# Row sums of attention brought to queries on partitions by 32-column products with four columns of the identity, in a step of their own

## The chip, the cores and the metric

The kernel runs on one core of one Trainium2 chip. The metric is the device time of one execution in microseconds (us): the median over the runs shown. A page of one profiled execution and its trace stand beside it.

## The reference, cut to what matters

Sixteen graphs (B = 16), each with 1024 nodes of 256 features and an integer adjacency matrix, pass through two layers. The first is a graph transformer with masked self-attention of 8 heads of 32 features, in which queries, keys and values are the same normalized rows; the second is a graph attention layer with one score per pair of nodes. Cut to the part around the change:

```
h = relu(layernorm(x))
n = layer_norm(h, gamma1, beta1)              # queries = keys = values, 8 heads of 32
scores = einsum("bhqd,bhkd->bhqk", n, n) / sqrt(32)
attn = softmax(where(adj > 0, scores, -inf))  # over k
h = h + einsum("bhqk,bhkd->bhqd", attn, n)    # heads side by side again
x = x + h + gelu(layer_norm(h, gamma2, beta2) @ W1 + b1) @ W2 + b2
...                                           # then the second layer
```

The softmax's division is what the change touches: for every query and head, the weighted sum of values is divided by the row sum of the exponentials.

## The kernel before, in words

The path that runs here is `fast_path`. It is one long program without loops on the chip: Python generators emit the instructions of all sixteen graphs, and the order in which they are emitted is the order on each engine. `streams` holds six generators (attention, the MLP and second layer, preparation, loading of the next graph, masks, set-up), and the one with the least place goes next. While the attention of graph `b` runs, the MLP and the second layer of graph `b - 1` are emitted in between, a piece of some 1.75 us of TensorE's work at a time. `defer` sets a step aside until a clock of emitted work (`clock`) has passed a due time; `run_deferred` emits what is due.

Attention is done in units `(qh, g, kt)`: `qh` is a half of the queries (512), `g` a group of four heads, `kt` a block of 128 keys. A unit's scores stand transposed, keys on partitions and queries along the row: `scores` (L952) makes four heads' scores in PSUM, VectorE adds the mask (L973), ScalarE takes the exponential (L976). In the next unit `weigh` (L989) multiplies the exponentials with the values into `o`, where the four heads' 32 features lie on 128 partitions and the queries along the row. A DMA that adds (L1013) sums the exponentials over the key blocks.

After the eight key blocks of one `(g, qh)`, three steps follow, each in a later call of `go_on`, so that each has some microseconds to spare:

- `weigh` ends with a copy of `o` to `os` on VectorE (L1004);
- `total` multiplies the summed exponentials with ones (L901), which puts each head's row sums on 32 equal partitions of `den`, and ScalarE copies it to `ds` (L909);
- `finish` brings both to queries on partitions: four transposes of 128x128 of `ds` and four of `os` (L922), into two PSUM tiles `ptds` and `ptos`; a reciprocal of one column per head (L925), a product of outputs and reciprocals (L927) and an addition to `h` on GpSimd (L929).

`finish` is not called by `go_on` itself: it is put on the list `turns`, together with other transposes (of keys, `ptk`; of MLP inputs, `pty`; of second-layer inputs, `ptf`), with the number of PSUM tiles that it takes. `make_turns`, at the start of each unit, runs what there is room for:

```
was_totalled -> turns.append((2, lambda args=args: finish(*args)))
room = 3 - open_sums[0] - bool(summed) if open_sums[0] else 100
```

All these tiles, and those of the MLP and the second layer (`ph`, `po`, `pf`, `pa`, `pg`, `puT`, `lg`), come from one PSUM pool, `psm`, with three buffers; `open_sums` is 1 while a product that is only half summed holds one of them over a unit. A tile that is asked for takes the buffer that came free first, and its first instruction waits for the engine that read that buffer last.

Most products are made in quarters: `matmul` (L570) splits the 128 columns of the stationary operand into four of 32, each with its own 32 partitions of the output, and the four run side by side. Scores, `o` and `den` are split by hand into 64 and 32 columns. Only the transposes take the array whole, 128 by 128. The set-up makes two products of one moving column each, `p_w_a`, in the same quarters.

There are 16 x 2 x 2 = 64 calls of `finish`.

Of the kernel before, what the change touches and what calls it, by code (L numbers as in the profile page):

```python
# [9 lines left out]
F32 = mybir.dt.float32  # L10
# [6 lines left out]
P = 128  # L17
# [476 lines left out]
def fast_path(  # L494
# [28 lines left out]
    nc = tc.nc  # L523
    B, N, D = x.shape
    DFF = W1.shape[1]
    H, HD = 8, D // 8
    GH = 4
# [6 lines left out]
    TPH = QW // P  # L534
# [6 lines left out]
    const = pool("const", 1)  # L541
# [11 lines left out]
    smallp = pool("smallp", 3)  # L553
# [4 lines left out]
    def ps_tile(shape, name, dtype=F32):  # L558
        return psm.tile(shape, dtype, tag="ps", name=name)
# [36 lines left out]

    ident = const.tile([P, P], F32, name="ident")
    make_identity(nc, ident)
    ident8 = const.tile([P, P], FP8, name="ident8")
    nc.vector.tensor_copy(ident8, ident, saturate=False)  # L600
    ones = const.tile([P, HD], F32, name="ones")
# [131 lines left out]
    clock = [0.0]  # L733
    deferred = []

    def defer(us, f):
        deferred.append((clock[0] + us, len(deferred), f))

        return clock[0] + us

    def run_deferred(until=0.0):
        while True:
            due = [d for d in deferred if d[0] <= max(until, clock[0])]
            if not due:
                return
            d = min(due, key=lambda d: d[:2])
            deferred.remove(d)
            d[2]()
# [132 lines left out]
    turns = []  # L881

    open_sums = [0]

    def make_turns():
        room = 3 - open_sums[0] - bool(summed) if open_sums[0] else 100
        while turns and turns[0][0] <= room:
            n, f = turns.pop(0)
            room -= n
            f()  # L890
# [3 lines left out]
    scored, weighed, summed, totalled = [], [], [], []  # L894

    def total(b, qh, g, os, accs):

        den = ps_tile([P, QW], f"den_{b}_{g}_{qh}")
        for j in range(GH):
            for acc in accs:  # L900
                nc.tensor.matmul(  # L901
                    den[j * HD : (j + 1) * HD, :],
                    ones,
                    acc[j // 2][:, j % 2, :],
                    start=acc is accs[0],
                    stop=acc is accs[-1],
                )
        ds = tmpp.tile([P, QW], F32, tag="w2", bufs=3, name=f"ds_{b}_{g}_{qh}")
        nc.scalar.copy(ds, den)  # L909
        totalled.append((b, qh, g, ds, os))  # L910

    finished = {}

    def finish(b, qh, g, ds, os):
        h = hs[b]
        finished[b, qh] = finished.get((b, qh), 0) + 1
        clock[0] += 1.0
        pts = []
        for n, c in (("ds", ds), ("os", os)):
            pt = ps_tile([P, TPH, P], f"pt{n}_{b}_{g}_{qh}")  # L920
            for t in range(TPH):
                nc.tensor.transpose(pt[:, t, :], c[:, t * P : (t + 1) * P], ident)  # L922
            pts.append(pt.rearrange("p t (j d) -> p t j d", d=HD))
        rl = smallp.tile([P, TPH, GH], F32, tag="rl", name=f"rl_{b}_{g}_{qh}")
        nc.vector.reciprocal(rl, pts[0][:, :, :, 0])  # L925
        ot = tmpp.tile([P, TPH, GH, HD], F32, tag="w2", bufs=3, name=f"ot_{b}_{g}_{qh}")
        nc.vector.tensor_mul(ot, pts[1], rl.unsqueeze(3).to_broadcast([P, TPH, GH, HD]))  # L927
        ho = h[qh][:, :, g * P : (g + 1) * P]
        nc.gpsimd.tensor_add(ho, ho, ot.rearrange("p t j d -> p t (j d)"))  # L929

    def attention(b, st):
# [84 lines left out]
        for u in units:  # L1016
            make_turns()
            es, rest_of_weights = scores(*u)
            go_on()
            rest_of_weights()  # L1020
            qh, g, kt = u
            if kt == 0:
                sums[g, qh] = es
            else:
                for i in range(2):
                    defer(2.0 + 1.5 * i, lambda u=u, e=es[i], i=i: add_up(*u, e, i))
            scored.append((weigh, (*u, es)))
            yield

    def go_on():  # L1030
        was_weighed, was_summed, was_totalled = weighed[:], summed[:], totalled[:]
        for l in (weighed, summed, totalled):
            l.clear()
        if scored:
            f, args = scored.pop()
            f(*args)
        summed.extend(was_weighed)
        for args in was_summed:
            total(*args)
        for args in was_totalled:  # L1040
            turns.append((2, lambda args=args: finish(*args)))
        clock[0] += 2.0

    def close_attention():
        for _ in range(4):
            make_turns()
            go_on()
            yield
        make_turns()
        quarters[0] = False  # L1050
# [436 lines left out]
def kernel(tc, x, adj, gamma1, beta1, *rest):  # L1487
    nc = tc.nc
    D = x.shape[2]
    with tc.tile_pool(name="flags", bufs=1) as flags:  # L1490
        flag = flags.tile([1, 1], I32, name="bounded")
        redo = flags.tile([1, 1], I32, name="redo")
        with tc.tile_pool(name="bound", bufs=1) as pool:
            r = pool.tile([1, 2, D], F32, name="bound_rows")
            for i, src in enumerate((gamma1, beta1)):
                nc.sync.dma_start(
                    r[:, i, :], bass.AP(tensor=src.tensor, offset=src.offset, ap=[[0, 1], [1, D]])
                )
            m = pool.tile([1, 2], F32, name="bound_max")
            nc.vector.tensor_reduce(  # L1500
                m, r, axis=mybir.AxisListType.X, op=ALU.max, apply_absolute_value=True
            )
            s = pool.tile([1, 1], F32, name="bound_sum")
            nc.vector.tensor_scalar_mul(s, m[:, 1:2], math.sqrt(32.0))
            nc.vector.scalar_tensor_tensor(s, m[:, 0:1], 16.0, s, op0=ALU.mult, op1=ALU.add)
            nc.vector.tensor_scalar(
                flag, s, math.sqrt(BOUND * math.sqrt(32.0)), None, op0=ALU.is_le
            )
        nc.vector.tensor_scalar(redo, flag, -1.0, 1.0, op0=ALU.mult, op1=ALU.add)
        bounded = nc.values_load(flag[0:1, 0:1], min_val=0, max_val=1)  # L1510
        with tc.If(bounded > 0):
            fast_path(tc, x, adj, gamma1, beta1, *rest, redo)
        again = nc.values_load(redo[0:1, 0:1], min_val=0, max_val=1)
        with tc.If(again > 0):
            general_path(tc, x, adj, gamma1, beta1, *rest)
# [28 lines left out]
```

## Time and profile before

| What | us |
|---|---|
| median of three runs | 3492.38 (3491.94 to 3497.32) |
| the profiled execution | 3488.4 |
| its span, first to last instruction | 3486.6 |
| TensorE (PE) busy | 3432.9 |
| VectorE (DVE) busy | 2759.6 |
| ScalarE (ACT) busy | 1858.0 |
| GpSimd (POOL) busy | 1415.0 |
| `ptds` transposes, 256 instructions, busy | 42.0 |
| `ptos` transposes, 256 instructions, busy | 38.8 |
| reciprocals L925, 64 | 15.9 |
| products L927, 64 | 44.3 |

PE is TensorE's matrix products and PEld its loads of stationary operands, which run under the products. An fp32 product leaves two records of each kind, a transpose one. "128*32" in a row is the part of the array that is used, rows by columns. The busy time of a group counts overlapped instructions once; the mean of one is its own duration. Idle time has the name of the instruction whose end released it, or "issue" where the profile shows no wait. All durations are of the one profiled execution.

### The profile page before, as it was taken

The numbers are of one execution on the slowest core, as the hardware profiler recorded it, in microseconds if no ns is written. First come the engines' busy times: TensorE is split into PE (matmuls) and PEld (weight loads), VectorE is DVE, ScalarE is ACT, GpSimd is POOL, SyncE is SP. The second block draws the span as 40 slices with busy tenths as digits, with TensorE's granted clock in tenths as the row PEclk, the third lists the DMA queues.
The fourth block names the chain that finished last, engine by engine and source line by source line (L and its number), as shares of the span: only waits on it lengthen the run. The fifth ranks groups of instructions, "written<-read, shape, count | busy, mean of one in ns | idle before, by whom it ended". The sixth has DMA issues, their size and how long they took to land.

```text
span 3486.6 us, 115512 instructions
## 1 busy us (share of the span) xinstructions
PE 3432.9 (98%) x50686; PEld 1634.1 (47%) x50686; DVE 2759.6 (79%) x5193; ACT 1858.0 (53%) x2184; POOL 1415.0 (41%) x1708
## 2 busy tenths in 40 slices
PE   6999999999999999999999999999999999999998
PEld 2244444444444444444444444444444444444477
DVE  6888788787877877888887887878878788887754
ACT  4555555555555555555555555555555555555522
POOL 3443443434434344443444534344344443534220
PEclk9999999999999999999999999999999999999999
DMA  7699989999899998989989899998999989899720
GB/s 186 148 184 165 189 165 186 181 191 187 163 186 175 191 181 169 182 171 189 196 170 182 168 185 186 184 188 160 190 177 192 185 165 182 169 190 184 148 62 14
DMA packets 281892, 598.33 MB, mean 172 GB/s; under 512 B 94882, under 2 KB 130084, under 8 KB 281380
## 3 DMA queue, kind: packets, MB, share of 16 engines
q0 software_dynamic: 124416, 453.04, 71.0%
q1 hardware_dynamic: 154276, 134.41, 15.1%
q8 instruction: 400, 6.55, 0.8%
q10 hardware_dynamic: 2688, 3.41, 0.3%
q14 instruction: 112, 0.92, 0.1%
HBM read 104.21 MB, written 16.78 MB: 35 GB/s over the span
## 4 chain that ended last, share of the span: by engine, by line
PE 91%; DMA 3%; DVE 3%; issue 1%; ACT 0%; POOL 0%; SPq 0%; ACTq 0%; POOLq 0%; DVEq 0%
PE s L952 15%; PE o L989 13%; PE pa L570 12%; PE ph L570 11%; PE po L570 11%; PE lg L570 10%; PE pg L570 3%; PE puT L570 3%; PE pf L570 3%; DMA acc<-e 2%; PE den L901 2%; PE pty L1119 1%; PE ptf L1195 1%; PE ptk L801 1%; PE pa L567 1%
## 5 line engine op out<-in xcount | busy, mean ns | idle before, releaser
L976 ACT ACTIVATE e<-e 128x1024 f32<-128x1024 f32 x852 | 896.1, 1057 | 958.7 <-DVE e L973 722.2
L1013 POOL DMA_DIRECT2D acc<-e x864 | 756.1, 892 | 1433.8 <-DMA acc<-e 635.4
L973 DVE TENSOR_TENSOR e<-s,mk 128x1024 f32<-128x1024 f32 x852 | 1002.4, 1217 | 181.0 <-PE s L952 153.2
L952 PE MATMUL s<-kT 32*64 32x512 f32 x8192 | 579.9, 616 | 4.0 <-DVE odd L973 3.2
L989 PE MATMUL o<-e,va 128*32 128x512 f32 x3456 | 461.8, 605 | 2.1 <-ACT e L976 2.1
L570 PE MATMUL pa<-gw,e 128*32 128x258 f32 x7648 | 453.4, 380 | 0.0
L570 PE MATMUL lg<-fT,uT 128*32 128x256 f32 x7680 | 447.4, 379 | 0.0
L570 PE MATMUL ph<-yT,w 128*32 128x256 f32 x7808 | 446.4, 379 | 0.0
L570 PE MATMUL po<-w,hid 128*32 128x256 f32 x7680 | 439.0, 379 | 0.0
L570 PEld LDWEIGHTS ph<-yT,w 128*32 128x32 f32 x7808 | 255.3, 110 | 211.7 <-issue 50.7
L570 PEld LDWEIGHTS pa<-gw,e 128*32 128x32 f32 x7648 | 249.7, 110 | 210.9 <-issue 56.7
L570 PEld LDWEIGHTS po<-w,hid 128*32 128x32 f32 x7680 | 250.1, 110 | 209.1 <-issue 58.5
L570 PEld LDWEIGHTS lg<-fT,uT 128*32 128x32 f32 x7680 | 250.0, 110 | 208.6 <-issue 43.4
L1243 DVE SCALAR_TENSOR_TENSOR e<-lg,gw,mk 128x256 f32<-128x256 f32 x512 | 223.0, 477 | 71.6 <-PE lg L570 61.1
L1249 ACT ACTIVATE e<-e,shift 128x512 f32<-128x512 f32 x256 | 182.9, 717 | 179.9 <-DVE e L1248 124.4
L1146 DVE TENSOR_TENSOR hid<-ph,b1c 128x512 f32<-128x512 f32 x256 | 175.9, 687 | 89.0 <-PE ph L570 77.4
L989 PEld LDWEIGHTS o<-e,va 128*32 128x32 f32 x3456 | 68.6, 108 | 353.6 <-issue 201.7
L976 ACT ACTIVATE acc<-acc 128x1024 f32<-128x1024 f32 x124 | 131.0, 1057 | 130.0 <-DVE acc L973 125.6
L1248 DVE SCALAR_TENSOR_TENSOR e<-e 128x512 f32<-128x512 f32 x256 | 191.9, 750 | 8.8
L952 PEld LDWEIGHTS s<-kT 32*64 32x64 f32 x8192 | 120.9, 130 | 164.8 <-issue 118.3
L973 DVE TENSOR_TENSOR acc<-s,mk 128x1024 f32<-128x1024 f32 x124 | 146.0, 1218 | 16.8 <-PE s L952 16.7
L793 POOL TENSOR_TENSOR nrm<-nrm,g 128x256 f32<-128x256 f32 x128 | 112.6, 880 | 62.8 <-DVE nrm L727 62.8
(145 smaller groups left out, 3825.5 us busy)
## 6 DMA issues: line engine op xcount, KB each, us to landing
acc<-e POOLq DMA_DIRECT2D x864, 512.0 KB, 6.1
adj<-in_adj_dram SPq DMA_DIRECT2D x248, 256.0 KB, 5.4
h<-in_x_dram SPq DMA_DIRECT2D x64, 256.0 KB, 5.8
xb<-in_x_dram SPq DMA_DIRECT2D x128, 128.0 KB, 4.9
out_dram<-z SPq DMA_DIRECT2D x128, 128.0 KB, 3.8
adj<-in_adj_dram SPq DMA_DIRECT2D x4, 512.0 KB, 7.0
mk<-mq SPq DMA_TRANSPOSE x128, 6.2
w<-in_L_gnn_W_dram ACTq DMA_DIRECT2D x2, 1024.0 KB
```

What stands on the lines that cost most here:

```text
L570: nc.tensor.matmul(out[c : c + HD], lhsT[:, c : c + HD], rhs, start=start, stop=stop)
L793: nc.gpsimd.tensor_mul(nrm, nrm, g1)
L901: nc.tensor.matmul(den[j * HD : (j + 1) * HD, :], ones, acc[j // 2][:, j % 2, :], start=acc is accs[0], stop=acc is accs[-1],)
L952: nc.tensor.matmul(sc[j // 2][c : c + P // 2, j % 2, :], kT[r, g, kt * P + c : kt * P + c + P // 2], kT[r, g, qs], start=j >= by_pe, stop= ...
L973: nc.vector.tensor_tensor(e, masked, mb, op=ALU.add)
L976: weights = lambda e=e, masked=masked: nc.scalar.activation(e, masked, AF.Exp, scale=SCALE)
L989: nc.tensor.matmul(o[j * HD : (j + 1) * HD, :], va[:, kt, (g * GH + j) * HD : (g * GH + j + 1) * HD], es[j // 2][:, j % 2, :], start=(kt = ...
L1013: nc.gpsimd.dma_start(sums[g, qh][i], e, accum_op=ALU.add)
L1146: nc.vector.tensor_tensor(hid[:, f0 : f0 + 2, :], ph, b1c[:, f0 : f0 + 2].unsqueeze(2).to_broadcast([P, 2, CW]), op=ALU.add,)
L1243: nc.vector.scalar_tensor_tensor(e[:, j, :], lg[:, j, :], gw[:, kt, D : D + 1], st[c // 2][:, kt // 2, qs, kt % 2], op0=ALU.add, op1=ALU.add,)
L1248: nc.vector.scalar_tensor_tensor(e, e, ALPHA, e, op0=ALU.mult, op1=ALU.max)
L1249: ready = defer(2.5, lambda: nc.scalar.activation(e, e, AF.Exp, bias=shift))
```

## The change

A constant `each_head` is added: columns 0, 32, 64 and 96 of the identity. `finish` is parted in two. `invert`, called straight from `go_on`, multiplies `ds` with `each_head` in 16 products, four per block of 128 queries: the stationary operand is 32 columns of `ds`, the moving one has four columns. The result holds, for 128 queries on partitions, the row sums of four heads side by side (the 32 equal partitions of each head are not summed: a column of `each_head` picks one). Its PSUM tile has 4 x 4 columns where there were 4 x 128. The reciprocal is set aside for 1.0 us of the clock. What is left of `finish`, the transposes of `os` and what follows, goes to `turns` and takes one PSUM tile.

```
+    each_head = const.tile([P, GH], F32, name="each_head")
+    nc.vector.tensor_copy(each_head, ident[:, ::HD])
...
-        room = 3 - open_sums[0] - bool(summed) if open_sums[0] else 100
+        room = 3 - open_sums[0] - bool(summed or totalled) if open_sums[0] else 100
...
-    def finish(b, qh, g, ds, os):
+    def invert(b, qh, g, ds, os):
+
+        pt = ps_tile([P, TPH, GH], f"ptds_{b}_{g}_{qh}")
+        for t in range(TPH):
+            for c in range(0, P, HD):
+                nc.tensor.matmul(
+                    pt[c : c + HD, t, :], ds[:, t * P + c : t * P + c + HD], each_head, start=True, stop=True
+                )
+        rl = smallp.tile([P, TPH, GH], F32, tag="rl", name=f"rl_{b}_{g}_{qh}")
+        ready = defer(1.0, lambda: nc.vector.reciprocal(rl, pt))
+        turns.append((1, lambda: finish(b, qh, g, rl, ready, os)))
+
+    def finish(b, qh, g, rl, ready, os):
         h = hs[b]
+        run_deferred(ready)
         finished[b, qh] = finished.get((b, qh), 0) + 1
-        clock[0] += 1.0
-        pts = []
-        for n, c in (("ds", ds), ("os", os)):
-            pt = ps_tile([P, TPH, P], f"pt{n}_{b}_{g}_{qh}")
-            for t in range(TPH):
-                nc.tensor.transpose(pt[:, t, :], c[:, t * P : (t + 1) * P], ident)
-            pts.append(pt.rearrange("p t (j d) -> p t j d", d=HD))
-        rl = smallp.tile([P, TPH, GH], F32, tag="rl", name=f"rl_{b}_{g}_{qh}")
-        nc.vector.reciprocal(rl, pts[0][:, :, :, 0])
+        clock[0] += 0.5
+        pt = ps_tile([P, TPH, P], f"ptos_{b}_{g}_{qh}")
+        for t in range(TPH):
+            nc.tensor.transpose(pt[:, t, :], os[:, t * P : (t + 1) * P], ident)
         ot = tmpp.tile([P, TPH, GH, HD], F32, tag="w2", bufs=3, name=f"ot_{b}_{g}_{qh}")
-        nc.vector.tensor_mul(ot, pts[1], rl.unsqueeze(3).to_broadcast([P, TPH, GH, HD]))
+        nc.vector.tensor_mul(
+            ot, pt.rearrange("p t (j d) -> p t j d", d=HD), rl.unsqueeze(3).to_broadcast([P, TPH, GH, HD])
+        )
...
         for args in was_totalled:
-            turns.append((2, lambda args=args: finish(*args)))
+            invert(*args)
```

In the order of instructions, the 64 groups of 16 products stand one piece of work (some 3.5 us of TensorE's) earlier than the transposes that they replace, right behind the unit's `o` products; the `os` transposes stay where they were. On VectorE the 64 reciprocals stand some instructions earlier. The other engines' instructions and their order are the same.

## The prediction

> **What bounds the kernel now.** I read the page's busy table first, then the chain that ended last, then the busy times by stretch.
>
> ```profile
> PE 3432.9 (98%) x50686; PEld 1634.1 (47%) x50686; DVE 2759.6 (79%) x5193; ACT 1858.0 (53%) x2184; POOL 1415.0 (41%) x1708
> ...
> PE 91%; DMA 3%; DVE 3%; issue 1%; ACT 0%; POOL 0%; SPq 0%; ACTq 0%; POOLq 0%; DVEq 0%
> ```
>
> TensorE is busy for 98% of the span and carries 91% of the chain. By stretches it is clearer still (columns: window, its length, busy time of PE, weight loads, DVE, ACT, POOL, granted clock, DMA share, GB/s):
>
> ```profile
> 215.00:3270.00 3055.00, 3050.64 (x46768) 1425.32 (x46768) 2474.66 (x4630) 1669.24 (x1956) 1288.67 (x1544) 1.00 0.92 180
> ```
>
> For 3055 of 3486.6 us TensorE is idle for 4.4 us in all; VectorE has 19% of its time free there. The reader is to see that what comes off TensorE's own instruction stream there comes off the end, as long as no other engine makes it wait. DMA at 0.92 is the one resource to watch: but of all waits of TensorE those on the DMA of the sums, at `den`, come to 6.3 us only.
>
> Next the step that is changed. Its transposes (count, then ns of one: least, median, most), and, from the list of who waited for them, the weight loads (PEld) of the next tile (us in total, times):
>
> ```profile
> L922 PE MATMUL ptds<-ident,ds x256: 272/273/329, 72.3 to 3345.7; 128*128 128x128 f32 x128
> ...
>   PEld ptos L922: 6.4, 14
> ```
>
> So there are 64 finishes with four `ds` transposes each, and in 14 of them the `os` transposes that follow sit waiting. The timeline of one of the 14 shows why:
>
> ```profile
> 335.67 0.87 DVE L1243 SCALAR_TENSOR_TENSOR e<-lg,gw,mk 128x256 f32<-128x256 f32 x2
> 335.79 0.42 PEld L922 LDWEIGHTS ptds<-ident,ds 128*128 128x128 f32 x4 [0.41 <-issue]
> ...
> 336.65 0.42 PEld L922 LDWEIGHTS ptos<-ident,os 128*128 128x128 f32 x4 [0.45 <-PE ptds L922]
> ```
>
> From the first `ptds` load to the first `ptos` load it takes 0.86 us here. In the ordinary case (next fence) it takes 0.38: so 0.48 us is a wait. It ends when VectorE's L1243 has read the `lg` tile (335.67 + 0.87 = 336.54): with three PSUM buffers in this pool, `ptos` gets the one that held that `lg`.
>
> For the price of the new instruction, the set-up holds one that is nearly the same: the 16 quarter products of `p_w_a`, with 32-column weights and one moving column, just ahead of the first finish (timeline: start us, us, engine, line, operation):
>
> ```profile
> 71.96 0.43 PE L570 MATMUL p_w_a<-a1c,stage 128*32 128x1 f32 x32
> ```
>
> The loads just after it are those of an ordinary finish, and of what follows:
>
> ```profile
> 72.33 0.42 PEld L922 LDWEIGHTS ptds<-ident,ds 128*128 128x128 f32 x4
> 72.71 0.47 PEld L922 LDWEIGHTS ptos<-ident,os 128*128 128x128 f32 x4
> 73.35 0.12 PEld L570 LDWEIGHTS <-ident 128*32 128x32 fp8e5 x8 [0.17 <-issue]
> ```
>
> The 16 fp32 products leave 32 records, two each (the transposes one each).
>
> **What the Trainium skill says.** (1) "TensorE: Matmul & The Clock Gate", section on LDWEIGHTS: a load's time goes by its columns, columns / 1.2 ns: 107 ns for 128, 27 for 32. The trace agrees: in the 72 us finish the four `ptos` matmuls span 0.60 us, less one's 0.272 is 0.328 for three steps, 109 ns each; and the 32 records of `p_w_a` come in eight groups of four, about 32 ns a group. (2) The same page, section "Wait — 56ns, not 53.3ns?": starts are never under about 25 ns apart however small the product. The trace differs: (0.43 - 0.173, the mean of one) us over 31 gaps is 8 ns, as four quarters run side by side; the trace decides. (3) "TensorEngine Tiling (Array Packing)", Key Properties: a change of tiling mode drains TensorE. The trace agrees: loads sit idle 0.41 us ahead of a group of 128-wide transposes and 0.17 after it. (4) "Perfetto Trace Analysis", Optimization Strategy: a gap that repeats on the saturated engine can mean too little PSUM for the next tile; the 14 equal waits are such a gap.
>
> **The change part by part.**
> *Four transposes go, per finish.* Eight of them and the changeover take 73.35 - 72.33 = 1.02 us from first load to the next operation's. Four alone are seen elsewhere (`pty`, loads, then those of the scores):
>
> ```profile
> 3320.76 0.42 PEld L1119 LDWEIGHTS pty<-ident,y 128*128 128x128 f32 x4 [0.41 <-issue]
> 3321.35 0.23 PEld L952 LDWEIGHTS s<-kT 32*64 32x64 f32 x16 [0.17 <-DVE l L1287]
> ```
>
> That is 0.59 us. Removed: 1.02 - 0.59 = 0.43 us. The mode changes stay, since the `os` transposes stay where they were.
>
> *16 quarter products come.* 0.43 - 0.173 = 0.26 us from first to last start in `p_w_a`, which includes a first group that starts slower; with that group's load hidden under the product before it, eight groups of 32 ns, 0.26. Four moving columns instead of one: a 256-column group costs 453.4 us / 7648 x 4 = 0.24 us (row L570 `pa`), so three columns cost about 3 ns, under the 32 ns of the loads. I take 0.27. They stand in `go_on` right behind the second `o` product, which is 128x32 as well, so no mode change comes with them. Bounds: 0.22 (seven steps) to 0.42 (each group as slow as the first step of `p_w_a`, whose second group of four starts 53 ns after its first). Net 0.16 us per finish; 64 x 0.16 = 10.2 us.
>
> *The 14 waits.* `ptos` would now take the buffer that `ptds` held, freed by a reciprocal that stands on VectorE ahead of that `lg`'s L1243. What is late next: L1243 comes 0.25 us later, but its buffer goes to a product some microseconds on. So 14 x 0.48 = 6.7 us go. Bound: nothing gained (the wait moves to another tile) to 6.7.
>
> *Waits added.* The products wait for the copy `ds` on ScalarE and for a buffer; behind them on TensorE stands everything. In the `g` 1, `qh` 0 finish:
>
> ```profile
> 486.77 0.57 ACT L909 COPY ds<-den 128x512 f32<-128x512 f32 x1
> ...
> 490.99 2.35 DVE L973 TENSOR_TENSOR e<-s,mk 128x1024 f32<-128x1024 f32 x2 [2.56 <-PE s L952]
> ...
> 491.76 1.93 PE L570 MATMUL pg<-wo,fT 128*32 128x258 f32 x32
> ```
>
> `ds` is done at 487.34 and needed at about 491.76, when the `o` products end and `pg` starts: 4.4 us to spare. Tightest is the `lg` after the two `pg`: it needs the buffer that the reciprocal frees, about 493.34 + 0.25 = 493.6, and wants to load at about 493.55. I charge 0.05 us x 15 = 0.8; bounds 0 to 3.
>
> *VectorE:* 64 reciprocals of 248 ns move up by some four to fourteen instructions; none is added. They queue behind a unit's mask additions, which end after the products. One 128x4 copy comes at the start, at most the 0.27 us of the 128x128 cast of the identity; VectorE idles 1.62 us for the first `h` just after. Charged at nothing. ScalarE, GpSimd and the DMA queues issue the same instructions in the same order: SP's and POOL's transfers pass nothing. `room` in `make_turns` and the clock's 0.5 shift no other step.
>
> Sum: 10.2 + 6.7 - 0.8 = 16 us. Against the profiled execution's own 3488.4 (span 3486.6 plus 1.8): 3472. The median of the runs shown, 3492.38, stands 4.0 higher; I carry the difference over: **3476**.
>
> **Rivals.** *A, the waits move (0.13):* the PSUM wait turns up at another product, as three buffers still serve all. For it: the pool is unchanged and the new tile is held longer. Against: each successor's buffer was read long before. Gain 10 - 0.8, 3483. *B, another limit (0.07):* VectorE or the DMA accumulation at 0.92 takes up what TensorE gives. For it: that share. Against: TensorE's 4.4 idle us. Time about 3491. *C, slower (0.08):* the small products do not overlap in the full stream. At the skill's 25 ns floor for each of 32 records, 0.80 us replace 0.43: 64 x 0.37 - 6.7 = +17 us, 3509. It decides from 0.43 + 6.7/64 = 0.53 us per finish, 17 ns a record. Against: `p_w_a` with 8. *D,* that the 16 products do not replace the transposes: no; the row sums stand repeated over 32 partitions, and four columns of the identity pick one of each.
>
> **How the numbers follow.** My forecast gets 0.72; its own range, from the bounds of 0.22 and 0.42 us, is 3472 to 3486. A lies within it. For 8 in 10, with a few us between sets of runs (3491.94 to 3497.32 were seen), I give 3469 to 3488. A measurement here can tell about 0.2%, 7 us. Faster by more: 0.72 and most of A, 0.83. Same: B and the rest of A, 0.09. Slower: C, 0.08.
>
> **What would show it.** Right: `ptds` as 2048 records with 32-column weights, starts 8 ns apart, 0.27 us a group; no idle ahead of them; no wait of `ptos` on L1243; TensorE's busy time 10 us lower or more; `ptos` row unchanged. Wrong: a gap ahead of `ptds` released by ScalarE or VectorE; gaps ahead of `ph`, `pg` or `lg` right after it; groups over 0.5 us.

## The result, and the profile after

| | before | changed |
|---|---|---|
| median of 20 runs each | 3491.15 us | 3481.33 us |
| ratio, with its interval | | 0.9974 [0.9966, 0.9983] |
| profiled execution: own time | 3488.4 us | 3478.05 us |
| its span | 3486.6 us | 3476.3 us |

The change gains 9.8 us by the medians (5.9 to 11.9 by the interval of the ratio) and 10.3 by the two spans, where 16 were forecast: the shortfall is clear of the noise. In all that follows the ratios are those of fast runs; one execution of `e2_own_step`, 5037.73 us at a granted clock of 0.655, is counted in its median and not in its ratio.

The page of the changed kernel, its busy table and its chain:

```profile
PE 3426.5 (99%) x52478; PEld 1651.3 (48%) x52478; DVE 2745.4 (79%) x5194; ACT 1857.2 (53%) x2184; POOL 1419.1 (41%) x1708
...
PE 93%; DMA 4%; DVE 1%; issue 1%; ACT 1%; POOL 0%; SPq 0%; ACTq 0%; POOLq 0%; DVEq 0%
```

The reader is to see that TensorE is still what the chain is made of, that its busy time is 6.4 us less, and that the share of DMA in the chain has gone from 3% to 4%. The stretch that the prediction looked at (window, length, busy PE, weight loads, DVE, ACT, POOL, clock, DMA share, GB/s):

```profile
215.00:3270.00 3055.00, 3053.18 (x48540) 1445.46 (x48536) 2468.05 (x4641) 1671.71 (x1960) 1294.22 (x1547) 1.00 0.93 180
```

TensorE is idle for 1.8 us of 3055 by this count. The new products, the reciprocal that reads them, and who waited for them (us, times):

```profile
L922 PEld LDWEIGHTS ptds<-each_head,ds x2048: 106/113/113, 68.1 to 3332.2; 128*32 128x32 f32 x187
L922 PE MATMUL ptds<-each_head,ds x2048: 169/173/193, 68.5 to 3332.2; 128*32 128x4 f32 x187
L926 DVE RECIPROCAL rl<-ptds x64: 246/248/258, 69.3 to 3333.2; 128x16 f32<-128x16 f32 x64
...
  DVE rl L926: 0.7, 2
  PEld pf L570: 0.2, 1
```

The row in which the `ptos` loads waited 14 times is gone. The transposes that are left have the duration they had:

```profile
L936 PE MATMUL ptos<-ident,os x256: 272/273/329, 72.1 to 3335.7; 128*128 128x128 f32 x128
```

The timeline of the finish that the prediction showed as one of the 14 (there at 335.67 to 336.65), some lines of it:

```profile
333.11 0.42 PE L922 MATMUL ptds<-each_head,ds 128*32 128x4 f32 x30
...
333.39 0.17 PE L922 MATMUL ptds<-each_head,ds 128*32 128x4 f32 x1
333.40 3.64 PE L570 MATMUL lg<-fT,uT 128*32 128x256 f32 x62
334.61 0.25 DVE L926 RECIPROCAL rl<-ptds 128x16 f32<-128x16 f32 x1
...
336.97 0.14 PEld L936 LDWEIGHTS ptos<-ident,os 128*128 128x128 f32 x1 [0.41 <-DVE ve_c L724]
```

30 records in 0.42 us, one of them 0.173: (0.42 - 0.173) / 29 is 8.5 ns a start. The `lg` products follow at once, and the load of `ptos` has only the 0.41 us of idle time that stands ahead of the other groups of 128-wide transposes too (0.41 in the prediction's lines).

What has grown is a wait that the prediction didn't list: VectorE's mask addition, which needs an `e` buffer that an adding DMA still reads (us in all, times, longest). In the waits of the kernel before:

```profile
DVE e L973 <- DMA acc<-e: 3.2, 3, 1.5
```

and in those of the changed one:

```profile
DVE e L986 <- DMA acc<-e: 10.9, 15, 2.2
```

The weight loads of `den`, which the prediction did list, wait 5.0 us for these DMAs where it was 4.2.

To see what each finish gains I took, from the traces, the time from the first `os` transpose of a finish to that of the next, and subtracted that of the kernel before. 50 of the 64 finishes are ordinary; 14 are those with the wait. Most steps repeat to 0.01 us, and a few are irregular (the one profile of the kernel before has irregular steps too, which come in with the sign turned):

| kernel (edits below) | ordinary finish | one of the 14 | span against before | VectorE waits on the adding DMA |
|---|---|---|---|---|
| changed | -0.13 to -0.16 | -0.55 | -10.3 | 10.9 (15) |
| changed, again | the same | -0.55 | -7.5 | 11.7 (11) |
| `e1_in_place` | -0.17 to -0.22 | +0.06 | -1.9 | 9.5 (13) |
| `e2_own_step` | +0.26 to +0.29 | -0.12 | +10.7 | 3.3 (4) |
| `e7_none` | -0.44 to -0.46 | -0.85 | -27.8 | 14.0 (15) |
| `e3_double` | +0.10 to +0.13 | -0.27 | +26.2 | 18.6 (20) |
| `e10_due_1` | -0.14 to -0.16 | -0.55 | -4.2 | 7.7 (12) |
| `e10_due_3` | -0.14 to -0.16 | -0.55 | +13.5 | 33.8 (27) |

For the changed kernel the repeating part alone is 50 x 0.145 + 14 x 0.55 = 15 us. Single steps in its trace go the other way by 0.5 to 1.5 us, and the irregular ones together take back the rest, 4 to 5 us.

### The profile page after: what moved, and what is told of

The parts are those of the page before. It is cut to its first block, busy times and chain, and to the rows that moved or that the text cites. A ratio compares the mean times of both kernels' runs of the same rounds, so it can differ in the third digit from the quotient of the medians.

```text
span 3476.3 us, 119036 instructions
## 1 busy us (share of the span) xinstructions
PE 3426.5 (99%) x52478; PEld 1651.3 (48%) x52478; DVE 2745.4 (79%) x5194; ACT 1857.2 (53%) x2184; POOL 1419.1 (41%) x1708
## 4 chain that ended last, share of the span: by engine, by line
PE 93%; DMA 4%; DVE 1%; issue 1%; ACT 1%; POOL 0%; SPq 0%; ACTq 0%; POOLq 0%; DVEq 0%
PE s L965 14%; PE o L1002 13%; PE pa L570 12%; PE lg L570 12%; PE ph L570 11%; PE po L570 11%; DMA acc<-e 3%; PE pf L570 3%; PE pg L570 3%; PE puT L570 3%; PE den L904 2%; PE pty L1132 1%; PE ptos L936 1%; PE ptk L804 1%; PE ptf L1208 1%; PE pa L567 1%
## 5 line engine op out<-in xcount | busy, mean ns | idle before, releaser
L570 PEld LDWEIGHTS lg<-fT,uT 128*32 128x32 f32 x7680 | 258.4, 110 | 190.1 <-issue 38.8
```

The costliest lines, as they stand in the source:

```text
L570: nc.tensor.matmul(out[c : c + HD], lhsT[:, c : c + HD], rhs, start=start, stop=stop)
```

## The experiments

Two theories were held against each other. **S**: the shortfall lies in the change's own steps; the products cost more, or the waits were worth less, than forecast. **D**: the steps are worth some 14 us, and some 4 of them are lost where the adding DMA, which does not get faster, ends late. Times are against the kernel before, run beside each.

### The products at the old place

The 16 products, but directly ahead of the `os` transposes, in the order and the due times of before:

```
-    def invert(b, qh, g, ds, os):
-        pt = ps_tile([P, TPH, GH], f"ptds_{b}_{g}_{qh}")
+    def finish(b, qh, g, ds, os):
+        clock[0] += 1.0
+        ptd = ps_tile([P, TPH, GH], f"ptds_{b}_{g}_{qh}")
...
-            invert(*args)
+            turns.append((2, lambda args=args: finish(*args)))
```

> The 16 quarter products with four identity columns stand where the four transposes of ds stood, in the same turn, just ahead of the os transposes; every other instruction keeps the order of the kernel before. Theory S (the step sum: TensorE's time passes to the end in full): an ordinary finish saves about 0.44 us of transposes against 0.30 us of products, 0.13 us, times 50 = 7 us; the 14 finishes whose os transposes wait for VectorE's read of lg gain nothing, since the end of that wait stays: about 3485 against 3491.5, ratio 0.998. Theory D (part of what TensorE saves is taken back by waits on the adding DMA, through the exponentials' buffers): 4 to 5 us, ratio 0.9987. Both: the waits of ptos stay 14 and grow to about 0.6 us each.

Measured: 3490.59 us, ratio 0.9997 [0.9985, 1.0008]. The interval leaves out the 0.998 of S and holds the 0.9987 of D. The 14 waits stay, as the list of who waited for `ptds` shows:

```profile
  PEld ptos L928: 8.7, 14
```

From the last product ahead of the step to the scores after it is 1.295 us in the 14 cases and 0.69 in the ordinary ones (of the last `ptds` product, here): a wait of 0.605, longer than the 0.438 of before, since TensorE arrives earlier. What the products save is eaten there: one of the 14 finishes is 0.06 us longer than before, the others 0.17 to 0.22 shorter. So the swap of transposes for products and the removal of the 14 waits are two gains, and the second comes from the move. The repeating part is 50 x 0.18 - 14 x 0.06 = 8 us, and the span shows 1.9 of them: already here VectorE's waits on the adding DMA have gone from 3.2 to 9.5 us.

### The move without the products

Four transposes of `ds`, as before, in the early step of their own:

```
-        pt = ps_tile([P, TPH, GH], f"ptds_{b}_{g}_{qh}")
+        pt = ps_tile([P, TPH, P], f"ptds_{b}_{g}_{qh}")
...
+            nc.tensor.transpose(pt[:, t, :], ds[:, t * P : (t + 1) * P], ident)
```

> The step of its own, early in go_on, but with four 128-wide transposes of ds as before in place of the products. Both theories: the 14 waits of ptos go (-6 us), but each finish has two more mode changes of TensorE around the early transposes: 0.68 us there for 0.44 saved, +0.24 x 64 = +15.6: in sum +9.5 us on the kernel before, ratio 1.0027. If the early place itself were what brings the gain, it would be at least as fast as the changed kernel, 0.9974.

Measured: 3501.74 us, ratio 1.0023 [1.0013, 1.0034]. The waits are gone (0.896 us from last product to scores in all four kinds of finish), but each finish has a second pair of changeovers between quarters and the whole array, 0.26 to 0.29 us net. This kernel is slower than before, and its VectorE waits on the adding DMA are those of before, 3.3 us: its repeating steps sum to 50 x 0.28 - 14 x 0.12 = 12 us, the span says 10.7, and the medians 9.3 where 9.5 were forecast. So nearly the whole sum of steps comes out where the waits have not grown. That fits D.

### The products twice

```
+        for _ in range(2):
             for t in range(TPH):
```

> The changed kernel with each group of 16 products issued twice into the same tile. Prices the products in the full stream. Theory S: 64 x 0.25 to 0.30 = +16 to +19 us on the changed kernel, so 3497 to 3500, ratio to before 1.002. Theory D: less than the added TensorE time comes out, as waits on the DMA shrink: +12 to +14, 3494, ratio 1.0007 to 1.0015.

Measured: 3515.73 us, ratio 1.0066 [1.0054, 1.0078]; 34 us over the changed kernel, where both theories expected half of that or less. The doubled group itself costs what was expected: the product after it starts 0.267 us later in each finish, 17 us in all, 8.3 ns for each of 32 records. Of the other 17 to 19 us (by the spans, against the two profiles of the changed kernel) two parts can be named. VectorE's waits on the adding DMA have grown to 18.6 us and those of the weight loads of `den` to 9.9 (after: 5.0). And TensorE stops eight times, for 7.2 us, with no wait in the record; the two profiles of the changed kernel have none and 0.4 us of that. One such stop, from the timeline:

```profile
1413.97 0.59 PE L570 MATMUL pf<-wo,fT 128*32 128x256 f32 x3
1416.08 0.84 PE L570 MATMUL pf<-wo,fT 128*32 128x256 f32 x11 [1.51 <-issue]
```

What TensorE lacked there isn't shown, and it stays open. Against the kernel before, the repeating steps sum to 50 x 0.13 - 14 x 0.27 = 3 us, and the span says 26.2. D had the waits on the DMA shrink in a longer stream, and they grew: in this D was wrong.

### No products

The reciprocal reads a constant, so the attention is not divided by its row sums; the step keeps its place, its tile of `rl` and its due time.

```
-                nc.tensor.matmul(
-                    pt[c : c + HD, t, :], ds[:, t * P + c : t * P + c + HD], each_head, start=True, stop=True
...
+        ready = defer(1.0, lambda: nc.vector.reciprocal(rl, big.rearrange("p (t j) -> p t j", j=GH)))
```

> The changed kernel without the 16 products; the reciprocal reads a constant of 1e6 instead, so the attention is not divided by its row sums. Theory S: -0.30 x 64 = -19 us on the changed kernel, 3462, ratio to before 0.992. Theory D: the DMA takes back more as TensorE gets faster: -8 to -13 us, 3468 to 3473, ratio 0.994 to 0.995, and VectorE's waits on the adding DMA grow from 11 us to 20 or more.

Measured: 3466.56 us, ratio 0.9930 [0.9913, 0.9946]. Against the changed kernel each finish is 0.30 us shorter, 19 us in all, and the span 17.5 (20.3 against its second profile). So the products cost 0.30 us each finish; nothing else in the repeating steps hangs on them. By the medians the difference is 14.8 us, and the interval holds the 0.992 of S as well as the 0.994 to 0.995 of D, so this run does not tell the two apart. It does not bear out D's growth either: by its steps this kernel is 50 x 0.45 + 14 x 0.85 = 34 us under the kernel before, by its span 27.8, so that some 6 us are lost, no more than in the changed kernel (4 to 5, and 7 in its second profile). VectorE waits for the adding DMA 14.0 us, where D had 20 or more:

```profile
DVE e L982 <- DMA acc<-e: 14.0, 15, 2.1
```

### Half of the adding DMAs

Only the first of a unit's two halves is added, in the kernel before and in the changed one, so half of the row sums are incomplete; ScalarE's copy to `ds` adds 1000.

```
-                for i in range(2):
+                for i in range(1):
                     defer(2.0 + 1.5 * i, lambda u=u, e=es[i], i=i: add_up(*u, e, i))
```

> The kernel before with every second adding DMA (the second pair of heads of each unit) left out, so that those heads' row sums are incomplete; 1000 is added to the sums when they are copied. Base for the pair. Theory S: TensorE-bound as before, within 5 us of 3491. Theory D: a few us faster, 3483 to 3488, as VectorE's and TensorE's waits on the DMA go.

> The changed kernel with the same DMAs left out and the same addition. Theory S: faster than its base by the same 10 us as with all DMAs. Theory D: faster than its base by the 14 us of the step sum (8.5 for the products, 6.1 for the waits, less 0.6), no wait of VectorE on the adding DMA left.

In both the kernel's second path, `general_path`, computed everything again after the fast one, so the total times (12102.11 and 12092.1 us) say little here: in the two profiles what comes after the fast path takes 8628.6 and 8634.0 us, which hides 5 us of the difference. The fast path is read from its last product, `pn`, whose start the tile's rows give. Of before with half the DMAs, and of the changed kernel with half:

```profile
L1462 PE MATMUL pn<-seen,ones x2: 166/166/166, 3470.5 to 3470.6; 128*1 128x4 f32 x2
```

```profile
L1475 PE MATMUL pn<-seen,ones x2: 166/166/167, 3456.8 to 3456.8; 128*1 128x4 f32 x2
```

The change is worth 3470.5 - 3456.8 = 13.7 us here. With all the DMAs the same product starts at 3478.8 and 3468.4 (3471.3 in the second profile of the changed kernel): 10.4 or 7.5. In that stretch the DMA share is 0.53 in both and VectorE waits for no adding DMA in either, and from one finish to the next hardly any step deviates: -0.13 to -0.17 in ordinary ones and -0.54 or -0.55 in the 14. This is what D says and S excludes, with one profile of each. The kernel before gains 8.3 us from having half the DMAs, the changed one 11.6 (or 14.5).

Where these gains lie can be read by taking each kernel's steps against those of its own kind with half the DMAs. The kernel before loses 8.1 us in this way, the changed one 12.4 and in its second profile 15.6, each in a dozen or fewer of the 63 steps. The first two steps and the last make up 8.4, 8.6 and 9.8 us of these: what the change adds to the loss, 4 to 6 us, lies in single steps in between. In some of them the row sums themselves wait, and the step is longer by nearly the same time (1.27 us of wait and 1.40 of step, in the changed kernel):

```profile
2120.28 0.11 PEld L904 LDWEIGHTS den<-acc,ones 128*32 128x32 f32 x2 [1.27 <-DMA acc<-e]
```

VectorE's waits are a poorer guide: in the changed kernel five steps that hold a wait for an adding DMA lose nothing. The pair has a rival that it leaves standing: with half the DMAs GpSimd has half the issues to make too, so the late landing of a DMA and the fullness of GpSimd's queue are not told apart.

### The changed kernel again

The same kernel beside the last pair, for a second profile.

> The changed kernel once more, on the same chip as the pair with half the DMAs: both theories 10 us under the kernel before, ratio 0.9974. If its second profile shows the waits of VectorE on the adding DMA at other places and again near 11 us, they belong to the changed kernel; if they are back near 3 us with the span the same, theory D falls.

Measured: 3484.87 us, ratio 0.9974 [0.9962, 0.9986]. The repeating steps are the same to 0.01 us and the irregular ones differ (2.7 us at the eleventh finish, 2.5 at the thirty-third): between the two profiles it is the lost part that varies. VectorE's waits are 11.7 us, so they belong to the changed kernel and not to one execution of it.

### The adding DMAs earlier and later

```
-                    defer(2.0 + 1.5 * i, lambda u=u, e=es[i], i=i: add_up(*u, e, i))
+                    defer(3.0 + 1.5 * i, lambda u=u, e=es[i], i=i: add_up(*u, e, i))
```

and 1.0 in place of 2.0 for the other.

> The changed kernel with every adding DMA put on GpSimd's queue one due-time unit earlier (1.0 + 1.5 i in place of 2.0 + 1.5 i); nothing is added or removed. Theory D (the changed kernel loses about 4 us at VectorE's and the row sums' waits for these DMAs): a DMA issued earlier lands earlier, VectorE's waits on it fall from 11 us to under 7 and the time by 1-4 us, to 3477-3480. Theory S: the waits may move, the time stays within 1.5 us of 3481. Rival: the issue reaches GpSimd's queue before the exponential it reads or the DMA before it is done, and the queue stands at it; the time grows by 1-10 us.

> The same, one unit later (3.0 + 1.5 i). Theory D: the DMAs land later, VectorE's waits on them grow above 15 us and the time by 3-10 us over 3481. Theory S: within 1.5 us of 3481.

Later: 3496.43 us, ratio 1.0012 [0.9999, 1.0025], 15 us over the changed kernel, where D had 3 to 10 and S nothing. Of TensorE's instructions none is added, and the repeating steps are those of the changed kernel; all is lost at irregular ones. Three of the five longest of these (4.3, 4.7 and 5.8 us over the kernel with half the DMAs) hold waits of VectorE for an adding DMA of 4.3, 3.7 and 2.8 us, and the waits in all have grown:

```profile
DVE e L986 <- DMA acc<-e: 33.8, 27, 4.3
```

Earlier: 3480.18 us, ratio 0.9965 [0.9952, 0.9978], waits of 7.7 us (12). The waits moved as D says; the time differs from the changed kernel's by less than its interval, as S had it too, and is the lowest of the kernels that do all the work. The profiled execution itself took 3484.17 us, with single steps of 4.6 and 2.5 us lost at other finishes. So it is shown that adding DMAs issued later cost time, and no gain is shown from issuing them earlier.

### Part of the adding taken to GpSimd

```
+            if b and kt == 1:
+                nc.gpsimd.tensor_add(sums[g, qh][i], sums[g, qh][i], e)
+                return
             nc.gpsimd.dma_start(sums[g, qh][i], e, accum_op=ALU.add)
```

> The changed kernel, with the adding DMAs of the second key tile (96 of the 864; batches 1 to 3) replaced by a GpSimd tensor_add of the same 128x1024, which costs GpSimd an estimated 2.6 us (twice the 1.28 us of its 128x512 product) in place of the 0.89 us of an issue. Theory D (about 4 us of the change's 14 are lost where VectorE's mask additions and the row sums wait for the adding DMAs): the DMA share of the steady stretch falls from 0.93 to about 0.84, VectorE's waits on the adding DMA from 11 us to under 4, the time from 3481 to 3475-3478. Theory S (the change is worth only 10 us by its own steps): the time stays within 1.5 us of the changed kernel's. Rival G (GpSimd's longer instructions hold up the issues behind them): VectorE's waits on adding DMAs grow and the time goes above 3485.

> The same replacement in the kernel before. Theory D: this kernel loses some 3 us on VectorE at these waits and 6 us at the row sums; it gains 1-5 us, and the two kernels with the replacement are 12-14 us apart, ordinary finishes coming 0.14 us closer together in the changed one and hardly any step going the other way by over 0.4 us. Theory S: no gain, and 10 us between the two. Rival G: slower than 3495.

Measured: 3551.72 us, ratio 1.0159 [1.0144, 1.0174], for the changed kernel with it, and 3557.26, 1.0177 [1.0162, 1.0191], for the one before: the rival G. The edit takes 120 of the 864 DMAs and not 96: it holds for all fifteen graphs after the first, four `(g, qh)` each and two halves. Rows of the changed kernel with it, of GpSimd's groups and of the waits:

```profile
L1027 POOL TENSOR_TENSOR acc<-acc,e 128x1024 f32<-128x1024 f32 x120 | 283.0, 2377 | 141.1 <-ACT e L989 134.9 <-PE s L965 6.3
```

```profile
DVE e L986 <- DMA acc<-e: 49.6, 35, 2.4
...
PE ph L570 <- ACT ds L912: 22.5, 14, 1.7
...
PE puT L570 <- ACT ds L912: 18.7, 13, 1.5
```

The DMA share of its steady stretch fell to 0.81, and VectorE waits longer for DMAs than at 0.93, so a smaller share alone does not end the waits. GpSimd's queue, which issues all these DMAs, now holds the additions too; that this makes them late is likely and not shown by itself. TensorE also waits 41 us for buffers that ScalarE's copy `ds` holds, which it didn't before. The pair can't tell D from S.

### The reciprocal of the wide row sums on VectorE

A kernel with no row-sum transposes or products: VectorE takes the reciprocal of all 128x512 of `den`, GpSimd multiplies `os` with it, and VectorE adds the transposed outputs to `h`.

```
-        nc.scalar.copy(ds, den)
+        nc.vector.reciprocal(ds, den)
+        nc.gpsimd.tensor_tensor(os, os, ds, op=ALU.mult)
```

> A version without any product or transpose of the row sums: den has each head's sums on the same 32 partitions as that head's outputs, so VectorE takes the reciprocal of den (128x512) into ds, GpSimd multiplies os by ds ahead of the transposes, and VectorE adds the transposed outputs from PSUM to h. TensorE loses the 0.30 us of products, 64 x 0.30 = 19 us. VectorE: 64 wide reciprocals in place of the narrow ones; the two narrow rows seen (1 column 164 ns, 16 columns 248) give 5.6 ns a column as an estimate, about 3 us each: 190 us more on an engine with some 580 us free, in lumps of 3 us that can hold up the mask additions. Theory S: 3462 if the lumps hide, ratio 0.992. Theory D: 3468 to 3475. If VectorE's lumps decide: slower than the kernel before, 3500 to 3600.

Measured: 3601.85 us, ratio 1.0308 [1.0286, 1.0331].

```profile
L912 DVE RECIPROCAL ds<-den x64: 3344/3347/3359, 66.3 to 3451.6; 128x512 f32<-128x512 f32 x64
```

3.35 us in VectorE's queue 64 times; TensorE then waits for it (34.4 us at `puT` alone). With 16 columns the same operation takes 0.248 us: as this kernel does it, bringing the row sums to queries first is worth its 0.30 us of TensorE.

### Where a late DMA reaches TensorE

Most of one irregular step of the changed kernel (0.9 of 1.4 us) can be followed in its timeline, lines of GpSimd, VectorE and the weight loads:

```profile
1820.36 0.86 POOL L1026 DMA_DIRECT2D acc<-e  x1 [5.14 <-DMA acc<-e]
1820.92 1.61 POOL L942 TENSOR_TENSOR h<-h,ot 128x512 f32<-128x512 f32 x1
...
1820.74 2.27 DVE L730 TENSOR_SCALAR y<-h,mv_c,rs_c 128x256 f32<-128x256 f32 x2
...
1826.40 2.35 DVE L986 TENSOR_TENSOR e<-s,mk 128x1024 f32<-128x1024 f32 x2
...
1827.90 0.21 PEld L965 LDWEIGHTS s<-kT 32*64 32x64 f32 x8 [0.41 <-DVE e L986]
...
1828.81 0.21 PEld L965 LDWEIGHTS s<-kT 32*64 32x64 f32 x8 [0.71 <-DVE e L986]
```

GpSimd's queue stands 5.14 us at the issue of an adding DMA, which must wait for the one before it into the same sums. The addition to `h` stands behind it: its operand `ot` was ready at 1818.56 (start 1817.88, 0.68 us long) and it starts at 1820.92. VectorE's two `y` instructions, which read `h`, take 2.27 us, where the median of one is 0.407; the mask additions behind them are late, and the scores wait for them: the 0.41 us ahead of the first eight loads are there in the kernel before too, the 0.71 ahead of the next eight are not. In the kernel before, at the same finish, it was GpSimd that waited for VectorE:

```profile
1825.59 1.28 POOL L929 TENSOR_TENSOR h<-h,ot 128x512 f32<-128x512 f32 x1 [1.56 <-DVE ot L927]
```

That the `y` instructions waited for this addition is inferred from the operands and the times; the record doesn't name their releaser.

## Why the prediction came out right, and where its sum was off

- **The transposes that go:** forecast 0.43 us. From the last product ahead of the step to the scores after it, the traces have 1.332 us before and 0.896 after in ordinary finishes: 0.436.
- **The products that come:** forecast 0.27, measured 0.30 (`e7_none`, and the delay of the product after them). Start to start they are as forecast (8.5 ns); the term left out the tail. The four quarters of the product that follows start one after the other, some 16 ns apart, where they start some 7 ns apart in the kernel before; why is not shown. 64 x 0.03 is 1.9 us of the shortfall. The Trainium skill's floor of about 25 ns between starts ("TensorE: Matmul & The Clock Gate", "Wait — 56ns, not 53.3ns?"), on which rival C stood, is not a floor for the whole stream when products run side by side in quarters: 8.5 ns here. Four records start some 7 ns apart and the next four about 31 ns after them, so whether the floor holds within one quarter is not shown.
- **The 14 waits:** they are gone, as said, because the `os` transposes now take a buffer that was read long before; `e1_in_place` keeps them, and its repeating steps sum to 8 us in place of 15; `e2_own_step`, which moves the step without the products, has none. In size 1.770 - 1.332 = 0.438 us each and not 0.48, 0.5 us in all.
- **Waits added:** forecast 0.8 us, in 15 finishes at `lg`. In the trace there is one, 0.58 us, at a `pg` of the first pass. That the size is near is luck: the place and the count were wrong.
- **VectorE, GpSimd, ScalarE at nothing:** the reciprocal costs TensorE nothing that shows (248 ns, and the longest wait for it or for its tile in the rows above is 0.7 us in all, VectorE's own).
- **The step that was missing:** "DMA at 0.92 is the one resource to watch", the prediction said, and then weighed it by TensorE's waits at `den` alone and made it an all-or-nothing rival. It should have been a term of the sum. By its own steps the change is worth 8.5 + 6.1 - 0.6 = 14.0 us (64 x 0.133, 14 x 0.438, the wait added; the table's steps, which leave the last out, give 15); with half of the adding DMAs 13.7 are there, with all of them 10.4 in one profile and 7.5 in another. So 3 to 6 us are taken back at the adding DMAs: at the row sums, at VectorE's additions and in GpSimd's queue. How the loss goes with TensorE's speed is not shown. It did not grow when the products were left out, and it grew when they were doubled, so a TensorE that needs its buffers sooner does not explain it.
- **A mark that was ill chosen:** "TensorE's busy time 10 us lower or more". The 6 us of waits were idle time and could not show in it; 64 x 0.133 = 8.5 us could, and it fell by 6.4.

So of the 16 us forecast, 2 were mis-sized in the products and waits, and about 4 were lost at the DMA. That the range, 3469 to 3488, held the time is in this part luck: it was drawn from the bounds on the products' price and took in rival A, and the loss came at the resource of rival B, whose 3491 lay outside it.

## What to carry to other kernels

When TensorE's stream gets shorter in a kernel whose other resources have little room, sum the steps, and then look at the waits of every other engine on that resource, not only at the bound engine's: a late transfer can take back a part of the gain. In every kernel of the table whose mask additions waited more than before, the time came out worse than the sum of steps, whether it got faster (15 us by the steps against 10.3, 8 against 1.9) or slower (3 against 26); where the waits stayed as they were, the sum nearly held (12 against 10.7). To prove such a loss, thin out the resource in both kernels and see whether their difference grows to the sum of the steps.

## What the runs showed of the hardware that was not expected

- Quarter products of 32 columns with four moving ones start 8.3 to 8.5 ns apart per record, so 16 more of them in fp32 cost 0.27 us (`e3_double`), and the group with its tail 0.30 (`e7_none`).
- The changeover to 128-wide transposes depends on what runs ahead of it: their first load comes 0.307 us after the start of the last product of 256 columns, and 0.101 after that of a product of four (`e1_in_place`).
- TensorE had stops of up to 1.5 us with no wait in the record in the kernel with doubled products, 7.2 us in all; unexplained.
- VectorE's reciprocal of 128x512 from PSUM takes 3.35 us, 6.5 ns a column, where a mask addition of 128x1024 takes 1.22.
